# Degree counts moved into the dilation, attention weights prepared first, first convolution tiles filled during the dilation, stores on ACT's queue

## The chip, the cores and the metric

The kernel runs on one core of a Trainium2 chip as a single program. The metric is the device time of the program in microseconds (us). The engines are TensorE (PE; its weight loads are shown apart as PEld), VectorE (DVE), ScalarE (ACT), GpSimd (POOL) and SyncE (SP). DMAs are issued from SP, ACT and POOL, each on a queue of its own.

## What is computed

Sixteen graphs (matrices) of 1024 nodes, with 128 features each, go through four layers. The change touches the first, and the preparation of the second, third and fourth.

```python
# layer 0 for every graph b
h = relu(layernorm(x))
kept = dilate(adj)            # row by row; a row's removals also clear its column
deg = clip(sum(kept, axis=-1), 1, None)
for l in (1, 2, 3):
    agg = (kept @ h) / deg
    o = agg @ Wr[l] + h @ Wx[l] + b[l]
    h = batchnorm(relu(o / norm(o)))      # statistics over all graphs
x = x + concat(h1, h2, h3) @ Wl + bl
# layers 1 to 3, each on relu(layernorm(x)), with the same adj:
#   attention with log(adj) added to the scores (Wq, Wk, Wv, Wo),
#   graph attention (W, a), graph convolution (W, b), each added to x
```

## The kernel before

The program has three stages, each with its own memory pools.

**Dilation** (`dilate_plain`). The sixteen graphs stand in four quarters q of four graphs g each, all in SBUF as fp8 in the tiles `rows` (`M[q]`, 128 partitions x 8 KB per graph). POOL loads them from `adj`, with a cast, in pairs of DMAs (L726, L728), and the loads of later row blocks are gated. For each of eight row blocks s, `rounds(q)` finds the rows' removals by a fixed number of rounds, `DEPTH[s]` (three to nine): TensorE forms ranks in a PSUM bank y, DVE works out thresholds (L775 to L780), TensorE adds them (L828), ACT takes an absolute value (ya, L831), DVE compares (r, L834). A POOL product `pen` (L794) comes first. Each `bulk(q, g)` then applies the result to a graph's row block: TensorE sums (L870), ACT writes `y16` (L872), DVE updates the rows (L880), TensorE turns them (L891 to L894), ACT copies them into the columns (L896). After the last row block, the graph is stored to DRAM as `kept` from SP (L899), 1 MB.

The order is written by `in_order`. Each job is a generator that yields an engine, a duration, the time its input is ready, and a change in a pool of buffers; the planner picks the step that can start first, and records it. The engines' queues hold that order, and every engine works through its queue in order.

**Convolutions** (`convolutions_plain`). SP first loads the weights and vectors wr, wx, Wl, gam, bet, b6 (some twenty DMAs). The first pass, for every graph b, loads x (`xt`), normalises it on DVE, POOL and ACT into `h`, and calls `neighbours(b, h, True)`. That loads the graph's kept matrix into the tile `C`, of which there are two, and forms the degrees with 64 one-column matmuls (L996):

```python
if first:
    ps = pso.tile([P, HN], F32, name="o")[:, :NB]
    ...                       # 64 matmuls of C with ones
    nc.sync.dma_start(rdeg[b].rearrange("(c p) -> p c", p=P), rd[:, 0])
rdb = w2.tile([P, N], F32, name="rdb")
nc.sync.dma_start(rdb, rdeg[b][None, :].to_broadcast([P, N]))
```

The reciprocal degrees `rd` go to DRAM as `rdeg` in single values (L1004), and come back into every partition as `rdb` (L1006). TensorE transposes h (t, L1010; ACT copies it to hT, L1011), `Splitter` cuts h into three bf16 parts on ACT and DVE in turn (L676 to L679; it subtracts in place), and 48 matmuls g (L1021) form the aggregate in two PSUM banks. DVE multiplies each bank by rdb into aggT (L1023), which frees the bank. In two further passes, each layer's output (o, L1061 to L1068) is formed for every graph, and `neighbours` is called again, without the count. In this stage the order is the tile framework's; it lets later work pass where inputs and buffers allow. Tiles h, parts, rdb and xt have two buffers.

**Attentions** (`attentions_plain`). SP loads twelve kinds of weights and vectors, TensorE turns six matrices (L1175), two small products are formed (L1202, L1216), and then a second `in_order` plan runs the three attention layers. Its first work is the sum of x and the convolutions' result (L1328, L1331, from the spilled hT, `h_a`) and the adjacency rows a (SP L1283, ACT L1284).

Of the kernel before, what the change touches and what calls it, by code (L numbers as in the profile page):

```python
# [18 lines left out]
P = 128  # L19
# [681 lines left out]
def dilate_plain(tc, adj, eye, kept, unsettled):  # L701

    nc = tc.nc
    with ExitStack() as ctx:
# [148 lines left out]
        def bulk(q, g):  # L853

            m = M[q]
            for s in range(NB):
# [3 lines left out]
                y16 = bp.tile([P, N], F16, name="y16")  # L860
# [3 lines left out]
                for hf in range(2):  # L864
                    a = max(a, (yield "PE", 0.65, e, ("big", 1)))
# [13 lines left out]
                e = yield "DVE", 1.35, max(e, diagonal), 0  # L879
# [18 lines left out]
                if s == NB - 1:  # L898
                    nc.sync.dma_start(kept[q * G + g], m[:, g])  # L899

        with tc.manual_schedule(engines=set(ENGINES.values())):
            in_order([(9, 1e9, loads())] + [(q, 1e9, rounds(q)) for q in range(4)] + [(q + 100 + g / 9, 1e9, bulk(q, g)) for q in range(4) for g in range(G)],
                     {"big": 5, "y": 3})
# [10 lines left out]
def convolutions_plain(tc, x, eye, kept, rdeg, spill, final, Wr, Wx, bias, gamma, beta, Wl, bl):  # L914
    nc = tc.nc
    with ExitStack() as ctx:
# [3 lines left out]
        ap = ctx.enter_context(tc.tile_pool(name="c_adj", bufs=2))  # L920
# [5 lines left out]
        ident = cp.tile([P, P], F32, name="ident")  # L926
        nc.sync.dma_start(ident, eye)
        minus_half = cp.tile([P, NB], F32, name="minus_half")
        nc.vector.memset(minus_half, -0.5)
        ones = cp.tile([P, P], F32, name="ones")  # L930
        nc.vector.memset(ones, 1.0)
        ones8 = cp.tile([P, 1], F8, name="ones8")
        nc.vector.tensor_copy(ones8, ones[:, 0:1], saturate=False)
# [25 lines left out]
        wr = [matrix(w, f"wr{i}") for i, w in enumerate(Wr)]  # L959
        wx = [matrix(w, f"wx{i}") for i, w in enumerate(Wx)]  # L960
        wl = final[:3]
        for i, t in enumerate(wl):
            nc.sync.dma_start(t, Wl[i * D:(i + 1) * D])
        gam = [column(v, f"gam{i}") for i, v in enumerate(gamma)]
        bet = [column(v, f"bet{i}") for i, v in enumerate(beta)]
        b6 = [row6(v, f"b6_{i}") for i, v in enumerate(bias)]
        last = row6(bl, "bl6")
# [20 lines left out]
        def neighbours(b, h, first):  # L988
# [3 lines left out]
            if first:  # L992
                ps = pso.tile([P, HN], F32, name="o")[:, :NB]
                for i in range(NB):
                    for j in range(NB):
                        nc.tensor.matmul(ps[:, i:i + 1], C[:, j, i * P:(i + 1) * P], ones8, start=j == 0, stop=j == NB - 1)  # L996

                rd = small.tile([P, 2, NB], F32, name="rd")
                nc.vector.tensor_scalar(rd[:, 0], ps, 1.0, None, op0=ALU.max)
                nc.vector.reciprocal(rd[:, 0], rd[:, 0])  # L1000
                nc.vector.tensor_scalar(rd[:, 1], ps, 0.5, None, op0=ALU.is_ge)
                nc.vector.tensor_tensor(rd[:, 0], rd[:, 0], rd[:, 1], op=ALU.mult)
                with nc.allow_non_contiguous_dma(reason="1024 values"):
                    nc.sync.dma_start(rdeg[b].rearrange("(c p) -> p c", p=P), rd[:, 0])  # L1004
# [23 lines left out]
        for b in range(B):  # L1028
            xt = w2.tile([P, NB, D], F32, name="xt")
            nc.sync.dma_start(xt, natural(x[b]))  # L1030
            bs = small.tile([P, NB, 6], F32, name="bs")
            for c in range(NB):
                nc.vector.bn_stats(bs[:, c, :], xt[:, c, :])
            st = small.tile([P, 5, NB], F32, name="ln_st")

            nc.vector.tensor_tensor(st[:, 0], bs[:, :, 1], bs[:, :, 4], op=ALU.add)
            nc.vector.tensor_tensor(st[:, 1], bs[:, :, 1], bs[:, :, 4], op=ALU.subtract)
            nc.vector.tensor_tensor(st[:, 2], bs[:, :, 2], bs[:, :, 5], op=ALU.add)
            nc.vector.tensor_tensor(st[:, 1], st[:, 1], st[:, 1], op=ALU.mult)
            nc.vector.scalar_tensor_tensor(st[:, 2], st[:, 1], 32.0, st[:, 2], op0=ALU.mult, op1=ALU.add)  # L1040
            nc.vector.tensor_scalar(st[:, 2], st[:, 2], 1.0 / D, LN_EPS, op0=ALU.mult, op1=ALU.add)
            rsqrt(st[:, 3], st[:, 2])
            nc.vector.scalar_tensor_tensor(st[:, 4], st[:, 0], -0.5, st[:, 3], op0=ALU.mult, op1=ALU.mult)
            h = w2.tile([P, NB, D], F32, name="h")
            for c in range(NB):
                nc.scalar.activation(h[:, c, :], xt[:, c, :], AF.Relu, bias=st[:, 4, c:c + 1], scale=st[:, 3, c:c + 1])
            neighbours(b, h, True)

        wr_s, wx_s, constant = wr[0], wx[0], row_parts(b6[0], "const0")
        for l in range(3):  # L1050
            stats = kp.tile([P, 2 * B, 6], F32, name="stats")
            for b in range(B):
                if l:
                    rd6 = w2.tile([6, N], F32, name="xt")
                    nc.sync.dma_start(rd6, rdeg[b][None, :].to_broadcast([6, N]))
                    has = w2.tile([6, N], BF16, name="has")
                    nc.vector.tensor_scalar(has, rd6, floor, None, op0=ALU.is_gt)
# [24 lines left out]
                if l < 2:  # L1082
                    neighbours(b, h, False)
                else:
                    for hf in range(2):
                        t = pst.tile([P, HN], F32, name="t")
                        for c in range(4):
                            nc.tensor.transpose(t[:, c * P:(c + 1) * P], h[:, 4 * hf + c, :], ident)
                        nc.scalar.copy(hT[b][:, hf * HN:(hf + 1) * HN], t)
# [49 lines left out]
def attentions_plain(tc, x, spill, final, adj, deg, trouble, eye, Wq, bq, Wk, bk, Wv, bv, Wo, bo, W2, a2, W3, b3, out, scores, bound, reach):  # L1139
    nc = tc.nc  # L1140
    with ExitStack() as ctx:
# [29 lines left out]
        def turned(w, name):  # L1171
            n = w1.tile([P, HN], F32, name="rden")[:, :P]
            nc.sync.dma_start(n, w)
            ps = bank()
            nc.tensor.transpose(ps[:, :P], n, ident)  # L1175
            t = cp.tile([P, P], F32, name=name)
            nc.vector.tensor_copy(t, ps[:, :P])
            return t

        def column(v, name, scale=None):  # L1180
            t = cp.tile([P, 1], F32, name=name)
            with nc.allow_non_contiguous_dma(reason="128 values, once"):
                nc.sync.dma_start(t, v[:, None])
            if scale is not None:
                nc.vector.tensor_scalar(t, t, scale, None, op0=ALU.mult)
            return t

        def everywhere(v, name):
            t = cp.tile([P, D], F32, name=name)
            nc.sync.dma_start(t, v[None, :].to_broadcast([P, D]))  # L1190
            return t

        wq, wk_ = turned(Wq, "wqT"), turned(Wk, "wkT")
        wv, wo, w3 = turned(Wv, "wvT"), turned(Wo, "woT"), turned(W3, "w3T")
        qscale = SCALE / SIGMA
        bqc, bkc, bvc = column(bq, "bq", qscale), column(bk, "bk"), column(bv, "bv")
        bor, b3r = everywhere(bo, "bor"), everywhere(b3, "b3r")

        bv_m = w1.tile([P, HN], F32, name="rden")[:, :P]
        nc.vector.tensor_copy(bv_m, bvc.to_broadcast([P, P]))  # L1200
        ps = bank()
        nc.tensor.matmul(ps[:, :P], bv_m, wo, start=True, stop=True)  # L1202
        nc.vector.tensor_tensor(bor, bor, ps[:, :P], op=ALU.add)

        abd = cp.tile([P, 8], F32, name="abd")
        nc.vector.memset(abd, 0.0)
        with nc.allow_non_contiguous_dma(reason="256 values, once"):
            for h in range(H):
                for k in range(2):
                    nc.sync.dma_start(abd[h * HD:(h + 1) * HD, 4 * k + h:4 * k + h + 1],  # L1210
                                      a2[h, k * HD:(k + 1) * HD][:, None])
        w2T = turned(W2, "w2T")
        w2x = cp.tile([P, D + 8], F32, name="w2x")
        nc.sync.dma_start(w2x[:, :D], W2)
        ps = bank()
        nc.tensor.matmul(ps[:, :8], w2T, abd, start=True, stop=True)  # L1216
        nc.vector.tensor_copy(w2x[:, D:], ps[:, :8])
# [406 lines left out]
def in_order(jobs, pools):  # L1624
# [11 lines left out]
    def tile_of(j):  # L1636
        bank = j["next"][3]
        return bank if isinstance(bank, tuple) else (first, bank)

    while True:  # L1640
        best = None
        for j in jobs:
# [5 lines left out]
            pool, change = tile_of(j)  # L1648
            start = max(free[engine], needs, min(pools[pool]) if change > 0 else 0.0)
# [10 lines left out]
        pool, change = tile_of(j)  # L1660
# [3 lines left out]
        if change > 0:  # L1664
            k = pools[pool].index(min(pools[pool]))
            pools[pool][k] = float("inf")
            j["held"].setdefault(pool, []).append(k)
        elif change < 0:
# [117 lines left out]
```

## Time and profile before

| | us |
|---|---|
| median of three runs | 4152.04 (4149.99 to 4153.77) |
| profiled execution | 4155.19 |
| its span, first to last instruction | 4153.5 |
| last row copy of the dilation ends | 666.4 |
| first g of the convolutions starts | 688.8 |
| last g of the first pass ends | 996.9 |
| last DVE work of the convolutions | 1717.8 |
| first sum L1331 of the attentions | 1738.9 |

| whole span | PE | PEld | DVE | ACT | POOL |
|---|---|---|---|---|---|
| busy us | 3495.4 | 1998.0 | 2531.9 | 2397.5 | 782.0 |
| share | 84% | 48% | 61% | 58% | 19% |

The shares are averages over stages with different limits; what a part of the change is worth is read from its own stage. The page's clock row (PEclk) is the TensorE clock that was granted, as a share of full speed; DMA is the mean busy share of the sixteen DMA engines.

### The profile page before, as it was taken

How to read it: one execution, taken by the hardware profiler on the slowest of the kernel's cores; microseconds unless marked ns; L12 is line 12 of the kernel's file. 1: busy time of each engine (PE TensorE's matmuls, PEld its weight loads, DVE VectorE, ACT ScalarE, POOL GpSimd, SP SyncE). 2: the span in 40 equal slices, each digit the busy share in tenths (PEclk: the TensorE clock that was granted, in tenths of full speed). 3: DMA queues.
4: the chain of work that ended last, by engine and by line, in shares of the span. 5: the costliest groups of instructions: out<-in, count | busy, mean ns of one | idle time of the engine just before them, and what ended most of it. 6: DMA issues, size and time to landing. Idle time of an engine off the chain costs nothing.

```text
span 4153.5 us, 65822 instructions
## 1 busy us (share of the span) xinstructions
PE 3495.4 (84%) x26740; PEld 1998.0 (48%) x26740; DVE 2531.9 (61%) x4783; ACT 2397.5 (58%) x3945; POOL 782.0 (19%) x665
## 2 busy tenths in 40 slices
PE   5888885778999998578889898989988998989775
PEld 3555553345555556433455454545444544544433
DVE  4997773333334443325687678766776767687656
ACT  4777773333333334377657775777676667766540
POOL 7544521100000001111111121111112112111110
PEclk9899986889999999699999998999999999999887
DMA  9532233333332321322112212121222122111000
GB/s 86 33 21 15 14 123 106 112 115 103 134 125 103 124 108 54 118 72 65 53 62 67 77 52 67 67 69 44 67 77 67 47 67 77 52 62 52 26 16 17
DMA packets 212032, 292.12 MB, mean 70 GB/s; under 512 B 93948, under 2 KB 156168, under 8 KB 203528
## 3 DMA queue, kind: packets, MB, share of 16 engines
q1 hardware_dynamic: 127112, 245.61, 18.2%
q0 software_dynamic: 77568, 16.79, 6.7%
q10 hardware_dynamic: 7040, 25.43, 1.5%
q8 instruction: 211, 3.46, 0.3%
q14 instruction: 101, 0.83, 0.1%
HBM read 287.45 MB, written 50.66 MB: 81 GB/s over the span
## 4 chain that ended last, share of the span: by engine, by line
PE 52%; DVE 13%; ACT 6%; DMA 5%; issue 2%; POOL 2%; SPq 0%; ACTq 0%; POOLq 0%; DVEq 0%
PE acc L1418 9%; PE g L1021 8%; PE sum L1544 8%; PE t L1387 5%; PE sum L1598 4%; PE sum L1529 4%; DVE pm L1469 3%; DMA rdeg<-rd 2%; PE o L1067 2%; PE o L1068 2%; PE sum L1331 2%; ACT e L1395 1%; PE sum L1349 1%; DVE rden L1424 1%; PE sum L1269 1%
## 5 line engine op out<-in xcount | busy, mean ns | idle before, releaser
L1395 ACT ACTIVATE e<-t 128x1024 f32<-128x1024 f32 x512 | 507.9, 1022 | 488.1 <-PE t L1387 471.8
L1469 DVE SCALAR_TENSOR_TENSOR pm<-dst,minus,A 128x1024 fp8e4<-128x1024 f32 x512 | 676.1, 1349 | 7.3 <-DMA dst<-scores 7.2
L1021 PE MATMUL g<-C,parts 128*128 128x512 fp8e4 x2304 | 540.8, 390 | 76.4 <-DVE aggT L1023 72.3
L1382 ACT ACTIVATE t<-A 128x2048 f32<-128x2048 fp8e4 x256 | 481.9, 1883 | 3.9 <-ACT dst L1449 0.3
L1544 PEld LDWEIGHTS <-pm 128*128 128x128 fp8e4 x4096 | 347.4, 98 | 186.6 <-issue 164.8
L1544 PE MATMUL sum<-parts,pm 128*128 128x198 bf16 x4096 | 400.7, 251 | 26.2 <-DVE pm L1469 16.2
L1021 PEld LDWEIGHTS <-parts 128*128 128x128 bf16 x2304 | 226.3, 100 | 335.1 <-issue 86.9
L1418 PE MATMUL acc<-e,va 128*32 128x512 f32 x2048 | 332.5, 619 | 41.9 <-ACT e L1395 39.1
L1387 PE MATMUL t<-qT,kT 32*128 32x512 f32 x2048 | 304.9, 666 | 30.5 <-ACT t L1382 30.1
L1418 PE MATMUL acc<-e,ones_hd 128*32 128x512 f32 x2048 | 321.2, 602 | 0.0
L1023 DVE TENSOR_TENSOR aggT<-g,rdb 128x512 f32<-128x512 f32 x96 | 65.5, 690 | 377.1 <-PE g L1021 239.2
L1547 DVE TENSOR_REDUCE pos<-sum 128x132 f32<-128x396 f32 x256 | 144.8, 566 | 201.1 <-PE sum L1544 200.5
L1529 PE MATMUL sum<-parts,A 128*128 128x396 bf16 x1024 | 212.0, 352 | 42.9 <-DVE parts L1521 23.6
L1026 POOL TENSOR_TENSOR nrm<-nrm,minus_half 128x8 f32<-128x8 f32 x48 | 79.5, 1660 | 674.8 <-DVE nrm L1076 674.8
L1598 PE MATMUL sum<-A,gparts 128*128 128x512 fp8e4 x768 | 179.7, 388 | 25.0 <-ACT gparts L1581 17.6
L834 DVE TENSOR_TENSOR r<-ya,both 128x512 bf16<-128x512 f16 x184 | 146.8, 815 | 81.3 <-ACT ya L831 81.2
L1073 ACT ACTIVATE sq<-o 128x512 f32<-128x512 f32 x96 | 55.8, 598 | 227.6 <-PE o L1068 226.3
L880 DVE SCALAR_TENSOR_TENSOR rows<-y,thirty,rows 128x1024 fp8e4<-128x1024 f16 x128 | 171.2, 1347 | 24.5 <-ACT y L872 23.6
L1241 POOL TENSOR_TENSOR ln_st<-ln_st,minus_half 128x8 f32<-128x8 f32 x48 | 86.0, 1792 | 523.3 <-DVE ln_st L1239 389.3
L1529 PEld LDWEIGHTS <-A 128*128 128x128 fp8e4 x1024 | 94.7, 99 | 182.3 <-issue 105.0
L870 PE MATMUL big<-tri,rows 128*128 128x384 fp8e4 (+3 forms) x896 | 174.5, 314 | 1.3 <-ACT H L875 0.6
L883 POOL TENSOR_TENSOR own<-rows,lower 128x256 bf16<-128x256 fp8e4 x128 | 112.8, 891 | 323.7 <-DVE rows L880 229.1
(281 smaller groups left out, 6830.4 us busy)
## 6 DMA issues: line engine op xcount, KB each, us to landing
a<-in_adj_dram SPq DMA_DIRECT2D x128, 512.0 KB
C<-kept SPq DMA_DIRECT2D x48, 1024.0 KB
dst<-scores SPq DMA_DIRECT2D x64, 512.0 KB
rdb<-rdeg SPq DMA_DIRECT2D x48, 512.0 KB
spill<-hT ACTq DMA_DIRECT2D x48, 512.0 KB
kept<-rows SPq DMA_DIRECT2D x16, 1024.0 KB
h_a<-spill SPq DMA_DIRECT2D x64, 256.0 KB
xt<-in_x_dram SPq DMA_DIRECT2D x16, 512.0 KB
```

What stands on the lines that cost most here:

```text
L834: nc.vector.tensor_tensor(r, ya, both[:, 1, :, None].to_broadcast([P, G, P]), op=ALU.is_equal)
L870: nc.tensor.matmul(ps[:, k * P:], lhs, triF[:, :HN - k * P], start=k == 0, stop=k == 3)
L880: nc.vector.scalar_tensor_tensor(row, y16, hh[:, g:g + 1], row, op0=ALU.not_equal, op1=ALU.mult, saturate=False)
L1021: nc.tensor.matmul(ps, parts[:, k, j, :], C[:, j, cols], start=j == 0 and k == 0, stop=j == NB - 1 and k == 2)
L1382: nc.scalar.activation(s, A[b][:, k, None, cols].to_broadcast([P, H, HN]), AF.Copy, scale=16.0)
L1387: nc.tensor.matmul(s[:, hd], kT[r, k * P:(k + 1) * P], qT[r, cols], start=False, stop=True, skip_group_check=True)
L1395: nc.scalar.activation(es[:, hd:hd + 2], s[:, hd:hd + 2], AF.Exp, scale=SIGMA)
L1418: nc.tensor.matmul(ps[r], ones if one else va[:, k, r], es[:, hd], start=k == 0, stop=k == NB - 1)
L1469: nc.vector.scalar_tensor_tensor(pm[:, i, :], dst[hd], minus[:, i, hd:hd + 1], A[b][:, i, :], op0=ALU.is_ge, op1=ALU.mult, saturate=False)
L1529: nc.tensor.matmul(ps[:, :3 * H * W], A[b][:, i, j * P:(j + 1) * P], parts4[:, i, :, :, W:], start=i == 0, stop=i == NB - 1)
L1544: nc.tensor.matmul(ps[:, jj * 6 * W:(jj + 1) * 6 * W], pm[:, i, (j + jj) * P:(j + jj + 1) * P], flat(parts4[:, i, hd]), start=i == 0, stop ...
L1598: nc.tensor.matmul(ps, parts[:, k, m, :], A[b][:, m, cols], start=m == 0 and k == 0, stop=False)
```

## The change

Six things change.

1. The degree count moves to the end of each `bulk(q, g)`: 64 matmuls on the rows in SBUF, four DVE steps, one transpose of the 8 columns, and an ACT copy into `rd_row` (two buffers). `rdeg` is stored from ACT's queue in eight rows of 512 B. `neighbours` no longer counts and only loads `rdb`.
2. `kept` is stored from ACT's queue, not SP's, as each bulk ends.
3. The attention weights are loaded, turned and multiplied at the program's start, by `attention_weights`, on SP, ACT, TensorE and DVE; they go to DRAM as one array `ready_weights`, and the attentions load them with one DMA.
4. The tiles C and xt get pools that are opened ahead of the dilation. C for graphs 0 and 1 and x for graphs 0 and 1 are loaded while the dilation runs, and `norm_first` (job `beside`) normalises graph 0 in place there.
5. The convolutions' weights and vectors are loaded after the second graph's `neighbours` in the program's text, and x is loaded from POOL's queue.
6. `in_order` can take several buffer pools in one step, and the plan counts the six buffers of `y16`.

In the changed program's queues, TensorE has the counts of the first twelve graphs before the last quarter's final rounds, and the last four behind them, two ahead of the last two graphs' turning and two at the end. On SP, the loads of C for graphs 0 and 1 come ahead of wr and wx.

```diff
-                if s == NB - 1:
-                    nc.sync.dma_start(kept[q * G + g], m[:, g])
+            nc.scalar.dma_start(flat(kept[q * G + g]).bitcast(F32), flat(m[:, g]).bitcast(F32))
+            e = yield "PE", 1.8, a, ("big", 1)
+            ps = pp.tile([P, HN], F32, name="big")
+            turned, ps = ps[:NB, P:2 * P], ps[:, :NB]
+            for i in range(NB):
+                for j in range(NB):
+                    nc.tensor.matmul(ps[:, i:i + 1], m[:, g, j, i * P:(i + 1) * P], ones8[:, 0:1], start=j == 0, stop=j == NB - 1)
+            e = yield "DVE", 0.7, e, 0
+            rd = sp.tile([P, 2, NB], F32, name="rd")
...
+            e = yield "PE", 0.2, e, 0
+            nc.tensor.transpose(turned, rd[:, 0], ident)
+            yield "ACT", 0.3, e, ("big", -1)
+            row = sp.tile([NB, P], F32, name="rd_row", bufs=2)
+            nc.scalar.copy(row, turned)
+            nc.scalar.dma_start(rdeg[q * G + g].rearrange("(c p) -> c p", p=P), row)
...
-                    a = max(a, (yield "PE", 0.65, e, ("big", 1)))
+                    a = max(a, (yield "PE", 0.65, e, [("big", 1), ("y16", 1 - hf)]))
+                    if hf == 0:
+                        y16 = bp.tile([P, N], F16, name="y16")
...
-                     {"big": 5, "y": 3})
+            in_order([(9, 1e9, loads()), (1000, 1e9, beside)] + ...,
+                     {"big": 5, "y": 3, "y16": 6})
...
+def norm_first(tc, x, pool, h, minus_half):
+    nc.sync.dma_start(h, natural(x[0]))
+    t = yield "DVE", 3.2, 50.0, 0
...
+    yield "ACT", 2.3, t, 0
+    for c in range(NB):
+        nc.scalar.activation(h[:, c, :], h[:, c, :], AF.Relu, bias=st[:, 4, c:c + 1], scale=st[:, 3, c:c + 1])
...
         for b in range(B):
+            if b == 0:
+                h = h0
+            else:
+                xt = xp.tile([P, NB, D], F32, name="xt")
+                nc.gpsimd.dma_start(xt, natural(x[b]))
...
-            neighbours(b, h, True)
+            neighbours(b, h)
+            if b == 1:
+                wr = [matrix(w, f"wr{i}") for i, w in enumerate(Wr)]
+                wx = [matrix(w, f"wx{i}") for i, w in enumerate(Wx)]
...
+def attention_weights(tc, rp, ident, into, Wq, bq, Wk, bk, Wv, bv, Wo, bo, W2, a2, W3, b3):
...
+        for k, w in enumerate((Wq, Wk, Wv, Wo, W3, W2)):
+            (nc.sync, nc.scalar)[k % 2].dma_start(raw[:, k], w)
...
+        for k in range(6):
+            ps = pp.tile([P, P], F32, name="turn")
+            nc.tensor.transpose(ps, raw[:, k], ident)
+            nc.vector.tensor_copy(t[:, k * D:(k + 1) * D] if k < 5 else w2T, ps)
...
+        nc.sync.dma_start(into, t)
...
+        weights = cp.tile(list(ready_weights.shape), F32, name="weights")
+        nc.sync.dma_start(weights, ready_weights)
...
-        dilate_plain(tc, adj, eye, kept, unsettled)
+        ready_weights = dp.tile([P, 8 * D + 10], F32, name="ready_weights")
...
+            with tc.tile_pool(name="early", bufs=1) as yp, tc.tile_pool(name="c_adj", bufs=2) as ap, \
+                    tc.tile_pool(name="c_x", bufs=2) as xp:
...
+                attention_weights(tc, ap, ident, ready_weights, *weights)
+                dilate_plain(tc, adj, eye, kept, rdeg, unsettled, norm_first(tc, x, yp, h0, minus_half))
+                convolutions_plain(tc, x, ident, ap, xp, h0, minus_half, kept, rdeg, spill, final, *layer0)
```

## The prediction

> **What bounds the kernel now.** I read the table of stages first, then the chain of waits in the stage it singled out, then single instructions. The program has three stages: the dilation (0 to 667 us), the convolutions (to 1718) and the attentions. 0.2% of 4152 us is 8.3 us, about what a measurement of this kernel can tell from no change. Busy time by stage, all columns being engine busy us (with counts), granted clock, DMA share and GB/s:
>
> ```profile
> core 0: us, PE busy (x) PEld busy (x) DVE busy (x) ACT busy (x) POOL busy (x), PEclk, DMA share, GB/s
> 0.00:680.00 680.00, 510.61 (x5672) 346.03 (x5672) 499.73 (x1438) 452.56 (x889) 309.32 (x407) 0.89 0.48 53
> 680.00:1000.00 320.00, 241.87 (x1954) 129.41 (x1955) 109.44 (x399) 103.47 (x225) 25.72 (x16) 0.84 0.40 112
> 1000.00:1320.00 320.00, 302.46 (x1684) 182.56 (x1684) 124.69 (x227) 120.40 (x298) 31.64 (x20) 0.97 0.34 122
> ```
>
> From 1000 on TensorE is busy 302 of 320 us at clock 0.97: the second pass is bound by it. The first pass, 680 to 1000, is not: 242 of 320 us at clock 0.84, and no other engine is half busy. The chain of waits from 800 to 1020 says why:
>
> ```profile
> 817.87 0.20 DVE bs L1033
> 818.08 0.08 DVE rd L1002
> 818.17 10.28 DMA rdeg<-rd
> 828.46 4.33 DMA rdb<-rdeg
> ...
> 834.71 9.12 DMA rdeg<-rd
> ...
> 856.89 10.54 DMA rdeg<-rd
> 867.45 4.22 DMA rdb<-rdeg
> ...
> 873.59 10.39 DMA rdeg<-rd
> ```
>
> Each matrix's reciprocal degrees go to DRAM in about 10 us and come back in 4.3, and TensorE waits for aggT behind them. Two matrices take 38.5 us (g restarts at 837.59 and at 876.04). The waits agree: who waited, for whom, total us, times, longest.
>
> ```profile
> DVE aggT L1023 <- DMA rdb<-rdeg: 129.8, 14, 14.2
> ```
>
> Two more places matter, each in the timeline. The last row block of the dilation is copied at 666.4, the first g starts at 688.76. And in the attentions' start, SP issues 27 small loads and TensorE turns weights before the first sum L1331:
>
> ```profile
> 1718.11 0.33 SPq L1156 DMA_DIRECT2D ident<-in_eye_dram  x1
> ...
> 1730.20 0.90 SPq L1283 DMA_DIRECT2D a<-in_adj_dram  x2
> ...
> 1738.94 1.22 PE L1331 MATMUL sum<-final,h_a 128*128 128x128 f32 x4
> ```
>
> **What the Trainium skill says.** DMA: Bandwidth & Descriptors, Specifications, asks for at least 512 B per transfer for line rate. The trace agrees: 4 KB in pieces of 4 B takes about 10 us, the 512 KB broadcast 4.3. Its section on queues, rings and completion order says descriptors of one ring are consumed in order; so an rdeg store issued on ACT behind 1 MB kept stores waits for them. No run so far shows that. TensorE: Matmul & The Clock Gate, HAM oscillation, says idle gaps throw the clock back; the trace agrees (0.84 with the gaps, 0.97 without).
>
> **The change, part by part** (the sum is against the profiled execution, 4155.19 us; its span is 4153.5 and 1.7 lie around it. The median of the runs is 3.15 lower).
>
> *First pass: -103 (-80 to -128).* Before, first g to last g runs from 688.76 to 996.88, 308 us. Removed are 16 counts of 64 matmuls (1.74 us each) and the round trip inside the pass. In the changed instruction order two matrices form a unit: 96 matmuls g (44 took 9.50 us at full clock, 0.216 each: 20.7) and 16 transposes (8 took 0.87: 1.7), so 22.5 us if TensorE never waits. It will, once a unit: transposes read h, DVE subtracts in place after them, ACT casts, then g goes on. Without the rdb wait the trace's own sequence (872.51 to 876.04) costs 3.5 us, of which 2 are work counted above. ACT's order adds about 1: the next unit's h wait for statistics that stand behind aggT. I take 25 us a unit: 8 x 25 + 5 for a cold start = 205. Best is 8 x 22.5 = 180, worst 28.5 a unit = 228. Nothing else fills a unit: by the same trace DVE needs about 14 and ACT 13.5. C, rdb and x are 4 MB per unit, 160 GB/s, where 263 were moved at share 0.64 (600 to 620). x moves to POOL's queue, where one such issue costs about 0.9 us (L728); POOL is idle over 85% there.
>
> *Counts in the dilation: +15 (0 to 30).* Sixteen counts stay on TensorE, 1.74 us each plus a transpose. Twelve stand, in its order, before the last quarter's final rounds: 23 us. Idle time there is about 3.5 us (575 to 600, busy 86%) and 5 (600 to 617), so about 15 remain; it adds to the bound engine of a serial chain, and can do no better than vanish in the chain's own gaps. ACT gets 32 DMA issues at 0.33 us (as L1090) and 16 copies at 0.3; between 600 and 620 it is busy 18.2 of 20, so I count this cover as gone: part of the 15, its excess in the upper end. DVE's 0.7 us per count and h0 (3 us on DVE, 3.2 on ACT, 1.7 on POOL) fall in its 80 to 90% busy time: likewise. The buffer rule for y16 only orders; no ACT y waited for DVE in this trace, so 0 (-2 to 2, inside the ends).
>
> *Dilation start: +4 (0 to 10).* Weights, their store (0.5 MB) and two x are 2.1 MB, while row loads run at full DMA: pairs of 0.98 MB every 2.52 us (12.18, 14.71, 17.23), 390 GB/s. If all collides, 5.5 us, plus 640 pieces of 4 B. The engines' part is hidden: the first real product waits for pen on POOL until 29.6, and the weights should be turned by then. Without that cover it would cost what it exceeds.
>
> *Dilation end: +4 (0 to 6).* Two counts (3.5 us) stand on TensorE ahead of the last two matrices' transposes.
>
> *Start of the convolutions: -10 (-4 to -13).* 22.4 us from last copy to first g become about 12. C for matrices 0 and 1 and h for 0 lie ready, and about 20 small SP loads no longer precede them. What is late next: ACT's hT waits for all four last kept stores, since the new tiles lie where the rows were. Before, four stores issued 662.1 to 666.4 had landed by 674.5, 8 us after the last. Then hT, casts and subtractions, 4 us. The last two counts hide under the stores. wr and wx are not needed in the first units; SP passes 4 of them ahead of rdb, which is wanted half a g later.
>
> *Attentions' start: -9 (0 to -14).* 27 loads become 1; the a loads move from 1730.2 to about 1721.5, 0.43 us per issue. L1331 can move 13, so the adjacency stream sets 9. If later due work absorbs the head start it is 0.
>
> Sum: -103 + 15 + 4 + 4 - 10 - 9 = -99, 4056 profiled, **median 4053**. All good ends together give 3997, all bad ends 4114.
>
> **Rivals.** *TensorE-bound pass, chance 0.13.* The unit costs 22.5 and the chain's idle gaps absorb the counts: -128 + 0 + 4 + 4 - 10 - 9 = -139, median 4013. For it: 0.97 in the second pass. Against: the in-place subtraction above, with only two parts buffers.
>
> *The next wait, chance 0.10.* C has two buffers; a refill starts when g of the one before ends, and behind it queue rdb on SP. If C and rdb take 14 us instead of the 6 the trace shows (issue 738.61, first use 744.8), a unit costs 32: 256 + 5 is a saving of 47 instead of 103, median 4109.
>
> *Slower, chance 0.05: ACT stands at rd_row.* That tile has two buffers, so 14 of the 16 copies wait for the rdeg store two back, queued on ACT behind kept stores. While ACT stands, every ya and row copy behind it stands, and the last quarter's chain with it. The gain of 99 is gone at 7.1 us per copy; at 8.5 (119 us) the median is 4172. Against: four kept stores took 12.4 us, 3.1 each, mostly one or two stand ahead, and ACT has some 6 us of other work between.
>
> *It does nothing, 0.01:* only if the rdeg store still precedes each rdb in the pass.
>
> **Numbers.** Forecast 0.71, TensorE-bound 0.13, next wait 0.10, slower 0.05, nothing 0.01. Faster is 0.94, same 0.01, slower 0.05. The likeliest case's own ends are 3997 and 4114, each only if every term falls the same way; 4005 to 4110 holds both faster rivals and about 8 in 10.
>
> **What would show it.** In the changed profile: no chain through DMA rdeg in the convolutions; first g about 13 us after the last rows copy; units of 25 us; clock above 0.9 in the pass; last rows copy at about 690 rather than 666. A unit above 30 with waits on C, or long waits of rd_row for rdeg in ACT, would prove a rival; an attentions stage that ends as long after its start as before, but starts no earlier relative to the last layer, would void the -9.

## The result, and the profile after

The changed kernel takes **4034.64 us** (median of four runs, 4027.68 to 4039.04) against 4151.01 before: a ratio of 0.9719, with a 95% interval of 0.9702 to 0.9737, some 116 us saved where 99 were forecast. Its profiled execution took 4039.04 us, with a span of 4037.3, 116.2 under that of before. By stages, from the two profiled executions (us):

| | before | after | difference | forecast |
|---|---|---|---|---|
| last row copy of the dilation ends | 666.4 | 686.9 | +20.5 | +23 |
| from there to the first g | 22.4 | 7.3 | -15.1 | -10 |
| first g to the end of the pass's 768th g | 308.1 | 204.4 | -103.7 | -103 |
| from there to the last DVE work of the convolutions | 720.9 | 712.3 | -8.6 | 0 |
| the rest | 2435.7 | 2426.5 | -9.2 | -9 |

The table of stages of the changed kernel, with the same columns as before:

```profile
core 0: us, PE busy (x) PEld busy (x) DVE busy (x) ACT busy (x) POOL busy (x), PEclk, DMA share, GB/s
560.00:620.00 60.00, 55.40 (x981) 43.58 (x978) 39.58 (x135) 35.66 (x73) 10.21 (x14) 0.72 0.56 209
620.00:687.00 67.00, 48.93 (x678) 33.88 (x675) 29.18 (x95) 30.00 (x60) 9.87 (x10) 0.66 0.18 71
700.00:900.00 200.00, 190.70 (x937) 95.03 (x936) 102.83 (x324) 100.47 (x226) 37.58 (x29) 0.97 0.46 159
900.00:1152.00 252.00, 243.19 (x1345) 148.03 (x1344) 97.35 (x165) 97.60 (x240) 24.56 (x15) 0.98 0.36 128
```

In the first pass TensorE is now busy 190.7 of 200 us at clock 0.97, where it was 242 of 320 at 0.84; from 760 to 900 every 20 us slice is full. The price stands in the first row: from 560 to 620 TensorE is busy 55.4 of 60 us at a clock of 0.72, where the kernel before had 49.4 at 0.93. The chain of waits from 700 to 800 holds no rdeg. In its place, at the start of the pass alone, stands x:

```profile
725.33 6.96 DMA xt<-in_x_dram
732.32 1.66 DVE bs L1055 x8
735.01 1.67 POOL ln_st L1045
...
737.85 1.18 DVE bs L1055 x6
...
741.88 0.69 DVE aggT L1042
742.62 0.58 PE g L1040
...
747.04 20.33 PE g L1040 x92
...
771.02 19.86 PE g L1040 x92
```

The columns are start, duration, and what the chain went through. This load of x takes 7 us (the median of all is 4.9); its statistics (bs) stand on DVE ahead of aggT, which TensorE waits for; from 747 on g follows g. The timeline shows the steady units, two matrices each, 23.5 us apart:

```profile
794.65 20.02 PE L1040 MATMUL g<-C,parts 128*128 128x512 fp8e4 x92
...
818.15 20.02 PE L1040 MATMUL g<-C,parts 128*128 128x512 fp8e4 x92
```

The waits from 690 to 900 (total us, times, longest) say the same of the whole pass: the 129.8 us of aggT behind rdb are gone, DVE waits 31.7 us for x, and TensorE loses 9.2 us to aggT.

```profile
DVE bs L1055 <- DMA xt<-in_x_dram: 31.7, 11, 6.1
...
PE g L1040 <- DVE aggT L1042: 9.2, 3, 4.1
```

The timeline shows the two starts: that of the convolutions, and that of the attentions, whose last DVE work of the stage before ended at 1611.

```profile
686.32 0.59 ACT L898 CAST rows<-big 128x512 fp8e4<-128x512 f32 x1 [0.48 <-ACT rows L898]
...
692.50 1.07 ACT L1030 COPY hT<-t 128x512 f32<-128x512 f32 x2 [2.87 <-DMA kept<-rows]
...
693.47 1.15 ACT L676 CAST parts<-xt 128x512 bf16<-128x512 f32 x2
...
694.15 1.03 PE L1040 MATMUL g<-C,parts 128*128 128x512 fp8e4 x2 [2.49 <-DMA wr<-in_L_gnn_Wr_dram]
...
1617.91 1.06 ACT L1310 ACTIVATE A<-a 128x1024 fp8e4<-128x1024 f32 x1 [14.02 <-DMA a<-in_adj_dram]
```

The first g stands 7.3 us behind the end of the last row copy; 2.9 of these are hT's wait, which ACT has ahead of the casts (parts), for the last kept store. The trace puts the first g's own wait down to wr, which g doesn't read; what g needs is the first cast, and it is through at that time. In the attentions ACT's first adjacency block comes 7.1 us after the stage before, where it took 17.4 (1735.2 against 1717.8).

### The profile page after: what moved, and what is told of

Read it like the earlier page. It is cut to its first block, busy times and chain, and to the rows that moved or that the text cites. A ratio compares the mean times of both kernels' runs of the same rounds, so it can differ in the third digit from the quotient of the medians.

```text
span 4037.3 us, 65855 instructions
## 1 busy us (share of the span) xinstructions
PE 3474.4 (86%) x26756; PEld 1998.6 (50%) x26756; DVE 2527.9 (63%) x4782; ACT 2401.7 (59%) x3961; POOL 794.7 (20%) x680
## 4 chain that ended last, share of the span: by engine, by line
PE 58%; DVE 15%; ACT 7%; DMA 3%; issue 2%; POOL 2%; ACTq 0%; SPq 0%; POOLq 0%; DVEq 0%
PE g L1040 12%; PE acc L1444 9%; PE sum L1570 9%; PE t L1413 5%; PE sum L1624 4%; PE sum L1555 4%; DVE pm L1495 3%; PE o L1093 2%; PE sum L1357 2%; PE o L1094 2%; PE sum L1375 1%; ACT e L1421 1%; DVE rden L1450 1%; PE t L1029 1%; PE sum L1295 1%
## 5 line engine op out<-in xcount | busy, mean ns | idle before, releaser
L1040 PE MATMUL g<-C,parts 128*128 128x512 fp8e4 x2304 | 521.3, 381 | 15.4 <-DVE aggT L1042 9.2
L1413 PE MATMUL t<-qT,kT 32*128 32x512 f32 x2048 | 307.7, 672 | 31.7 <-ACT t L1408 31.3
L1624 PE MATMUL sum<-A,gparts 128*128 128x512 fp8e4 x768 | 178.0, 385 | 24.9 <-ACT gparts L1607 17.6
L1106 ACT ACTIVATE h<-o,nrm 128x128 f32<-128x128 f32 x384 | 105.7, 384 | 116.9 <-POOL nrm L1045 113.7
```

What stands on the lines that cost most here:

```text
L1040: nc.tensor.matmul(ps, parts[:, k, j, :], C[:, j, cols], start=j == 0 and k == 0, stop=j == NB - 1 and k == 2)
L1413: nc.tensor.matmul(s[:, hd], kT[r, k * P:(k + 1) * P], qT[r, cols], start=False, stop=True, skip_group_check=True)
L1624: nc.tensor.matmul(ps, parts[:, k, m, :], A[b][:, m, cols], start=m == 0 and k == 0, stop=False)
```

## The experiments

How much single executions differ is read from kernels that have a stage in common. The kernel before and row_store run the same instructions in the dilation, and its last row copies end at 666.4 in the first and at 660.9 in the second:

```profile
665.20 1.21 ACT L896 CAST rows<-big 128x512 fp8e4<-128x512 f32 x2 [0.54 <-PE big L891]
...
659.72 1.21 ACT L896 CAST rows<-big 128x512 fp8e4<-128x512 f32 x2 [0.53 <-PE big L891]
```

The three kernels with the changed dilation untouched (changed, x_four, after_again) end it at 686.9, 688.5 and 689.0. The first pass took 204.4 us in one execution of the changed kernel and 208.2 in the other. So a difference of up to 5.5 us at the last row copy, or 4 us in the pass, between two traces doesn't show an effect. The ratio of the changed kernel to the kernel before was 0.9719 in one set of runs and 0.9688 in another; ratios are compared inside one set of runs, and the first two sets below had no run of the changed kernel. The last three columns are when the last row copy ends, the first g starts and the convolutions end in the profiled execution:

| kernel | ratio to before | last row copy | first g | convolutions' end |
|---|---|---|---|---|
| before | 1 | 666.4 | 688.8 | 1717.8 |
| changed | 0.9719 (0.9702 to 0.9737) | 686.9 | 694.2 | 1610.8 |
| first set: row_store | 0.9796 (0.9778 to 0.9813) | 660.9 | 683.5 | 1633.6 |
| counts_back | 0.9905 (0.9887 to 0.9923) | 667.2 | 669.0 | 1706.8 |
| no_counts | 0.9634 (0.9607 to 0.9662) | 669.5 | 671.3 | 1583.6 |
| weights_back | 0.9730 (0.9713 to 0.9748) | 679.6 | 688.3 | 1604.1 |
| second set: stores_sp | 0.9686 (0.9660 to 0.9711) | 677.1 | 685.9 | 1602.3 |
| x_late | 0.9694 (0.9678 to 0.9710) | 681.9 | 689.9 | 1606.4 |
| x_four | 0.9699 (0.9683 to 0.9716) | 688.5 | 695.8 | 1614.2 |
| counts_late | 0.9689 (0.9672 to 0.9705) | 681.4 | 690.1 | 1609.4 |
| third set: after_again | 0.9688 (0.9675 to 0.9701) | 689.0 | 697.0 | 1612.8 |
| sp_xlate | 0.9652 (0.9639 to 0.9665) | 677.6 | 686.7 | 1610.2 |
| sp_xlate_clate | 0.9677 (0.9664 to 0.9690) | 678.3 | 687.2 | 1609.0 |
| sp_xlate_wlate | 0.9678 (0.9665 to 0.9691) | 681.5 | 690.1 | 1609.4 |

**row_store: the kernel before, with the store of the reciprocals in rows.**

```diff
+                turned, ps = ps[:NB, P:2 * P], ps[:, :NB]
...
-                    nc.sync.dma_start(rdeg[b].rearrange("(c p) -> p c", p=P), rd[:, 0])
+                nc.tensor.transpose(turned, rd[:, 0], ident)
+                row = small.tile([NB, P], F32, name="rd_row")
+                nc.scalar.copy(row, turned)
+                nc.sync.dma_start(rdeg[b].rearrange("(c p) -> c p", p=P), row)
```

> This is the kernel before with one edit: the reciprocal degrees are turned by TensorE and stored as 8 rows of 512 B instead of 1024 pieces of 4 B; counts and loads stay in the first pass. Theory A, the 4-byte pieces are most of the cost: the store falls from 10 us to about 2.5, the trip of some 7 us then lies beside the 10 us of g of the matrix before, and the first pass falls from 308 us to about 225 (it keeps 16 counts of 1.74 us), median about 4068. Theory B, any trip between two g costs, since it starts late: one wait of some 7 us stays per unit of two matrices, the pass takes about 265 us, median about 4108.

The first pass fell from 308.1 to 233.9 us, and the median by some 87. SP's timeline shows the trip, store and load in turn:

```profile
764.49 0.28 SPq L1007 DMA_DIRECT2D rdeg<-rd_row  x1
767.80 0.32 SPq L1009 DMA_DIRECT2D rdb<-rdeg  x1
...
780.88 0.30 SPq L1007 DMA_DIRECT2D rdeg<-rd_row  x1
782.15 0.33 SPq L1009 DMA_DIRECT2D rdb<-rdeg  x1
```

In all sixteen graphs the load is issued 1.2 to 3.3 us after the store, where 8.2 to 11.7 lay between. Where aggT waited 129.8 us for rdb in the pass, 18.8 are left (both from the waits, from 680 to 1000 and from 680 to 920). With the counts still in it, the pass now keeps TensorE busy:

```profile
core 0: us, PE busy (x) PEld busy (x) DVE busy (x) ACT busy (x) POOL busy (x), PEclk, DMA share, GB/s
760.00:900.00 140.00, 132.60 (x1205) 71.31 (x1204) 62.24 (x207) 61.83 (x142) 11.46 (x7) 0.99 0.42 141
```

So theory A holds, with a pass 9 us longer than it said: 74.2 of the 103.7 us that the change gains in the pass come from the form of the store alone, with the counts and the trip left where they were. The Trainium skill (DMA: Bandwidth & Descriptors, Specifications) asks for 512 B or more per transfer; here the trace agrees: from the store's issue to the load's, the same 4 KB take some 2 us in rows of 512 B and some 10 in pieces of 4 B.

**counts_back: the changed kernel, with the counts in the pass again, in 4 B pieces.**

```diff
-            e = yield "PE", 1.8, a, ("big", 1)
-            ... # count, reciprocals, transpose, copy and rdeg store of bulk()
+            if first:
+                ... # as in the kernel before: 64 matmuls of C, rd, rdeg on SP
```

> This is the changed kernel with the counts put back into the first pass, stored in 4-byte pieces on SP; C, x and h of the first matrices stay prefetched, the kept stores stay on ACT's queue, and the weights stay ready. Theory A, moving the counts is the change's whole gain in the pass: the pass is back at about 300 us, the dilation ends some 14 us earlier (last row copy near 673), median about 4115 to 4125. Theory B, the prefetched tiles and the short list of loads on SP carry a good part of it: median under 4080.

The pass took 316.4 us, no less than before, and the median lay at 4121.9, as theory A had it: the prefetched tiles carry only the start, which is even shorter here (1.8 us from the last row copy to the first g). But this edit brings back two things at once, the counts and the store in 4 B pieces, and row_store shows that most of the loss is the store. So it doesn't show that moving the counts is the gain. The dilation ended at 667.2, with its first dT at 57.0. That is level with the kernel before (666.4, first dT at 50.5), but 6.3 us behind row_store (660.9, first dT at 50.7); whether the late start is absorbed stays open.

**no_counts: the changed kernel without the counts.**

```diff
-            e = yield "PE", 1.8, a, ("big", 1)
-            ... # count, reciprocals, transpose and copy
-            nc.scalar.dma_start(rdeg[q * G + g].rearrange("(c p) -> c p", p=P), row)
+            nc.scalar.dma_start(rdeg[q * G + g].rearrange("(c p) -> c p", p=P), even)
```

> This is the changed kernel without the counts: their 16 x 64 matmuls, the reciprocals, the transposes and the copies are left out, and every stored reciprocal is the constant 1/32; the stores stay. It sizes the counts in the dilation. Theory A, as in the prediction: they cost about 10 us in the body and 4 at the tail, so the last row copy is near 673 instead of 687 and the median near 4021. Theory B, the gaps absorb them and the later end comes from the later start: the last row copy stays at 682 or later, median 4030 to 4035.

`even` holds the constant 1/32, so the stages after the first pass see other values than in the changed kernel.

```profile
core 0: us, PE busy (x) PEld busy (x) DVE busy (x) ACT busy (x) POOL busy (x), PEclk, DMA share, GB/s
560.00:620.00 60.00, 43.65 (x413) 28.17 (x413) 39.35 (x102) 41.21 (x82) 12.94 (x17) 0.87 0.61 230
620.00:670.00 50.00, 31.45 (x234) 17.89 (x232) 18.40 (x63) 19.59 (x36) 4.25 (x5) 0.60 0.13 50
```

Beside the rows of the changed kernel: TensorE does 75 us of work there instead of 104, and the last dT comes at 653.1 instead of 669.3. In these two traces the counts cost 16.2 us up to the last dT, 17.4 up to the last row copy, and 22.9 up to the first g (671.3 against 694.2), more than theory A had. Counted from the first kept store, where the counts begin, the last row copy ends after 112.7 us without them and after 127.2 with them, the latter in both executions of the changed kernel. The last 5.5 are order, as ACT's timeline in this kernel shows:

```profile
669.38 0.63 ACT L676 CAST parts<-xt 128x512 bf16<-128x512 f32 x1
...
678.24 1.07 ACT L1015 COPY hT<-t 128x512 f32<-128x512 f32 x2 [5.27 <-DMA kept<-rows]
```

Here the casts stand on ACT ahead of hT, so hT's wait of 5.3 us for the kept stores holds nobody, and g starts 1.8 us after the last row copy. In the changed kernel the casts stand behind it. The span is 37.7 us shorter than that of the changed kernel, 27.2 of it by the convolutions' end; the attentions, which see other values here, took 2416 us instead of 2426.5. That part stays open.

**weights_back: the attentions' weights loaded in the attentions again.**

```diff
-                attention_weights(tc, ap, ident, ready_weights, *weights)
...
-        nc.sync.dma_start(weights, ready_weights)
+        wq, wk_ = turned(Wq, "wqT"), turned(Wk, "wkT")
+        ... # and the rest, as in the kernel before
```

> This is the changed kernel with the attentions' weights loaded and turned at the attentions' start, as before. Theory A: the attentions' start costs 9 us more and the dilation begins some 3 us earlier (first dT near 53.5 instead of 56.9), of which nothing or little is left at its end: median about 4041. Theory B, a later start of the dilation carries to its end: 9 minus 3, median about 4038, and the last row copy 3 us earlier than 687. Theory C, the adjacency stream sets the attentions' start: within 3 us of 4035.

The ratio, 0.9730, overlaps the 0.9719 of the changed kernel's first runs and lies above the 0.9688 of the third set; as these are different sets of runs, they don't settle which is faster. The trace shows two opposite effects. The attentions' first adjacency block comes 15.7 us after the stage before, instead of 7.1:

```profile
1619.79 1.06 ACT L1351 ACTIVATE A<-a 128x1024 fp8e4<-128x1024 f32 x1 [22.63 <-DMA a<-in_adj_dram]
```

And the dilation's first dT comes at 51.8 instead of 56.9, its last row copy 7.3 us earlier, the way theory B had it. The early weights gain 8.6 us at the attentions' start and cost 5.1 us at the first dT, where the changed dilation's three executions lie within 0.6 us (56.6 to 57.2). How much of that is left at the dilation's end can't be read from one trace, when two executions of one dilation end 5.5 us apart.

**x_late: the first x issued on ACT at 100 us of planned work.**

```diff
-    nc.sync.dma_start(h, natural(x[0]))
-    t = yield "DVE", 3.2, 50.0, 0
+    t = yield "ACT", 0.4, 100.0, 0
+    nc.scalar.dma_start(h, natural(x[0]))
+    t = yield "DVE", 3.2, t + 8.0, 0
```

> This is the changed kernel with one edit: the first matrix's x is issued on ACT's queue, after about 100 us of the dilation's planned work, instead of on SP at 14 us. Theory A, this 512 KB is what holds up the row loads between 20 and 28 us (two of them 4.9 us apart instead of 2.5) and a late start is carried to the dilation's end: first dT near 52 instead of 56.9, last row copy near 682 instead of 687, median some 5 us under the changed kernel's. Theory B, the weights' loads and turns hold it up: first dT stays at 56 or later and nothing is gained.

The first dT came at 56.1, as theory B had it: x doesn't set the start. The last row copy came 5.0 us earlier, as theory A had it, but two executions of one dilation lie as far apart, so a gain isn't shown. The edit does more than move x: the plan orders the later work differently (the first kept store is issued at 568.8 instead of 559.7), and the statistics of x leave DVE's first 100 us (39 us of its work from 30 to 100 become 35).

**x_four: four tiles for x in the first pass.**

```diff
-                xt = xp.tile([P, NB, D], F32, name="xt")
+                xt = (xp, w2)[b // 2 % 2].tile([P, NB, D], F32, name=("xt", "h")[b // 2 % 2])
...
-                h = w2.tile([P, NB, D], F32, name="h")
+                h = xt
```

> This is the changed kernel with x's norm written in place, so that four tiles of x rotate in the first pass instead of two of x and two of h. Theory A, the cold start of the pass waits for x, whose refill stands behind h's release: the third x is issued near 692 instead of 698, the fourth near 693 instead of 704, and the stretch from the first g to the start of the steady units, 694 to 747 now, shrinks from 53 us to about 44; median some 9 us lower. Theory B, the cold start is set by ACT's and DVE's own order of work, or by the clock: it stays at 50 us or more, and the median within 3 us.

The wait for x went, and others came:

```profile
711.43 0.38 PE L1040 MATMUL g<-C,parts 128*128 128x512 fp8e4 x1
718.47 0.58 PE L1040 MATMUL g<-C,parts 128*128 128x512 fp8e4 x1 [6.66 <-DVE aggT L1042]
...
763.72 7.03 PE L1040 MATMUL g<-C,parts 128*128 128x512 fp8e4 x24 [2.22 <-DVE aggT L1042]
```

The second unit took 25 us instead of 32, but the first one waited 6.7 us for aggT, and later units wait for aggT too; the pass took 207.9 us, as in the second execution of the changed kernel. Its ratio doesn't stand apart from the others of its set. The cold start isn't the refill of x alone: DVE's order of work, with statistics of later graphs and DVE's waits of 1.4 to 1.6 us for POOL ahead of aggT, gives the next wait.

**stores_sp: the kept and rdeg stores on SP.**

```diff
-            nc.scalar.dma_start(flat(kept[q * G + g]).bitcast(F32), flat(m[:, g]).bitcast(F32))
+            nc.sync.dma_start(flat(kept[q * G + g]).bitcast(F32), flat(m[:, g]).bitcast(F32))
...
-            nc.scalar.dma_start(rdeg[q * G + g].rearrange("(c p) -> c p", p=P), row)
+            nc.sync.dma_start(rdeg[q * G + g].rearrange("(c p) -> c p", p=P), row)
```

> This is the changed kernel with the kept and rdeg stores issued on SP instead of ACT. Theory A, the other queue is what lets C be fetched early: on SP the two C loads stand behind the last kept stores, so that they start near 690 instead of 564, and the first g comes some 5 us after 694; ACT is freed of 32 issues of about 0.33 us; median within 5 us of the changed kernel's or a few us above. Theory B, the ACT issues are on the dilation's chain: last row copy some 5 to 10 us before 687, median lower by that.

Theory A is wrong: SP takes the C loads between the stores, at 565 and 580 us in its timeline.

The last row copy comes at 677.1, 9.8 us earlier than in the changed kernel, as theory B had it, but not all of that is the moved issues. Up to the first kept store both kernels run the same instructions, and this execution is 4.7 us ahead there:

```profile
554.98 2.30 SPq L900 DMA_DIRECT2D kept<-rows  x2
```

In the changed kernel:

```profile
559.69 0.35 ACTq L900 DMA_DIRECT2D kept<-rows  x1
```

From there to the end of the last row copy it takes 122.1 us, where both executions of the changed kernel take 127.2. So 5.1 us are left for the move of the issues. What an issue costs ACT is seen in two pieces of its timeline. With the stores on SP the next copy starts 0.14 us after the small copy of rd_row:

```profile
604.12 0.24 ACT L917 COPY rd_row<-big 8x128 f32<-8x128 f32 x1
604.26 0.57 ACT L898 CAST rows<-big 128x512 fp8e4<-128x512 f32 x1
```

In the changed kernel:

```profile
612.01 0.24 ACT L917 COPY rd_row<-big 8x128 f32<-8x128 f32 x1
612.28 0.29 ACTq L918 DMA_DIRECT2D rdeg<-rd_row  x1
612.62 0.59 ACT L898 CAST rows<-big 128x512 fp8e4<-128x512 f32 x1 [0.36 <-ACT rd_row L917]
```

This issue takes 0.29 us, and ACT's next copy starts after it is through: 0.61 us from the start of one copy to the start of the next, with ACT idle for 0.36. The Trainium skill (DMA: Bandwidth & Descriptors, Issuing engines are not separate DMA queues) says that issuing from several engines saves only issue time on the sequencer; here the move to ACT spent it on an engine that the dilation's chain goes through.

**counts_late: the twelve early counts held back, in halves.**

```diff
+            while q < 3 and (3, NB - 1) not in begun:
+                yield
-            e = yield "PE", 1.8, a, ("big", 1)
+            e = yield "PE", 0.95, a, ("big", 1)
...
+                if i == NB // 2:
+                    e = yield "PE", 0.95, e - HOP, 0
```

> This is the changed kernel with the twelve counts of the first three quarters held back until the last quarter's last round has begun, each in two halves of 32 matmuls, so that they stand in the gaps of that serial chain, where TensorE is busy 12 of 20 us. Theory A, a count costs what it adds to a busy TensorE: in the gaps, some 2 us in each of nine rounds of the chain, 18 of the 28 us vanish, and the last row copy is near 677 instead of 687; median some 9 us lower. Theory B, in the chain each count's reciprocals and copies on DVE and ACT and the longer gap delay the next step as well: last row copy at 687 or later.

```profile
core 0: us, PE busy (x) PEld busy (x) DVE busy (x) ACT busy (x) POOL busy (x), PEclk, DMA share, GB/s
620.00:640.00 20.00, 20.00 (x510) 17.78 (x508) 7.75 (x47) 3.72 (x10) 0.00 (x0) 0.59 0.02 5
```

The last row copy came at 681.4, 5.5 us earlier, where theory A had 10 and theory B none; two executions of one dilation differ by as much, so neither is shown. The gaps were overfilled: the plan put 96 count matmuls into each step of the chain, TensorE is busy 20 of 20 us there, and a step takes 5.2 us where the steps after the last count take 3.1. At the convolutions' end 1.4 us are left.

**after_again, and three combinations.** The edits are those above; sp_xlate_wlate also turns the weights into a planned job, behind a fill of their tile at 100 us of planned work.

> The changed kernel itself, so that the three kernels of this call stand beside it on one chip: 0.972 of the kernel before, as its runs showed, last row copy at 687, first g at 694.

> The changed kernel with the kept and rdeg stores on SP and the first x issued late on ACT. Theory A, the two gains are of different stretches and add up: last row copy some 14 us before 687, near 673, the first g near 681, the median some 13 us under the changed kernel's. Theory B, both only shift the order of work in the last rounds of the dilation, each gives the other's gain: near 677, median 8 us under.

sp_xlate is faster than the changed kernel in the same set of runs: 4026.2 against 4040.3 us, and the intervals of their ratios don't meet. It has the lowest ratio of all versions that compute the same. Its last row copy comes at 677.6, where stores_sp alone had 677.1 and theory A 673; with single traces 5.5 us apart this leans to theory B without settling it. Its profiled span is 11.2 us shorter than that of after_again, of which 2.6 arose by the convolutions' end and 8.6 in the attentions, which the edit doesn't touch. So the lower time is shown, its full cause isn't.

> As the kernel with stores on SP and a late first x, and the twelve early counts held back into the last chain's gaps. Theory A, the counts' matmuls still cost on the busy stretch: 4 us less again, last row copy near 669. Theory B, with ACT freed of the issues the counts are cheap where the change put them, and the held-back counts lengthen the chain: last row copy 5 us or more after that of the kernel without them held back.

> As the kernel with stores on SP and a late first x, and the attentions' weights loaded and turned within the dilation, behind a fill of their tile at about 100 us of planned work, instead of before it. Theory A, what the start loses is the time of the weights' and x's pieces in the DMA engines beside the row loads: with both moved the first dT is near 51 instead of 56.9, and the last row copy 5 us before that of the kernel without this; median some 18 us under the changed kernel's. Theory B, the later work on DVE, TensorE and SP costs in the busy stretch what the start gains: no difference of more than 2 us at the last row copy.

Neither adds to sp_xlate; both medians lie above its own (4033.1 and 4036.1 us). Held-back counts left the last row copy about where it was (678.3), between both theories. Late weights brought the first dT to 51.0, as theory A had it, but the last row copy didn't come earlier (681.5): the start's gain isn't seen at the end. The 3.9 us by which it came later are less than two executions differ by.

## Why the prediction was right, and where its steps were off

The direction held, and so did the mechanism, that the round trip of the reciprocal degrees holds up the first pass. The measured time lies in the range; the forecast saving was 17 us too small. Some of the terms were right by luck.

- **First pass, -103: measured -103.7, but from two errors that cancel.** The units were put at 25 us, of which 2.5 were a wait of TensorE. In the trace they follow each other at 23.5 (794.65, 818.15, 841.65) with no wait, and that includes some output products: the next unit's casts are done while g runs. The cold start was put at 5 us. At 23.5 a unit the pass would take 188; it took 204.4, so the cold start costs about 16. In the trace x and its statistics on DVE hold it up; x_four, without the wait for x, had other waits and no shorter pass. The second execution of the changed kernel took 208.2 us with the same steady units, so the agreement with -103 to the microsecond is luck. The TensorE-bound rival was right for the steady units, and wrong in that the counts would vanish. The next-wait rival named the right kind of wait, but C: g never waited for C; x was late, and only in the first two units.
- **What the -103 consists of** the prediction took as one removal. The form of the store alone gives 74.2 (308.1 to 233.9). The other 29.5 are, by size, the counts' own TensorE time, 16 x 1.74 = 27.8; and the dilation pays 22.9 of them up to the first g. By this sum the move itself is worth some 7 us, and with the second execution's 208.2 us in the pass and first g at 697.0 nothing is left of it. So it isn't shown that moving the counts gains anything over storing them in rows; no run had the changed kernel's start with the counts in the pass and the store in rows, which would measure it.
- **Counts, +15, and dilation end, +4: 16.2 up to the last dT, and from there to the last row copy 17.6 us instead of 13.5 (+4.1).** The first is sized well, from a sum of TensorE's time. (The prediction read 5 us of idle time from 600 to 617; TensorE is busy 13.2 of these 17 us, so it is 3.8. The 15 stays.) That ACT's issues are part of it was said: from the first kept store to the last dT stores_sp takes 105.8 us, where both executions of the changed kernel take 109.6. Behind the last dT the prediction named the two counts alone. With the counts and the stores on SP that stretch takes 16.4 us, with the kept stores on ACT but no counts (counts_back) 14.8. So some 2.8 of the 4.1 us are the counts and 1.3 are ACT's issues, a term that it put at nothing there.
- **Dilation start, +4: 6.4 at the first dT (50.5 to 56.9).** What is left of it at the dilation's end isn't shown. The last dT of no_counts, which starts as late, comes at 653.1; with the early start it came at 652.9 in the kernel before and at 647.7 in row_store. Against the first nothing is left, against the second nearly all.
- **Convolutions' start, -10: measured -15.1, past the good end of the range (-13).** The step that failed is its price after the stores: 8 us for the landing and 4 behind it. The stores landed 5.5 us after the last row copy; hT waited for them, the casts follow in 1 us, and g starts before the subtractions are through.
- **The rest of the convolutions, 0 expected: measured -8.6.** It was left out. In the changed kernel 40 recorded output products (L1093, L1094) run inside the first pass, instead of 10; 30 at 0.11 us are 3.3 us that the second pass no longer has. Around the end of the first layer TensorE's waits fell from 7.0 us (1249 to 1261) to 3.0 (1161 to 1164). The remaining 1.3 us are less than single executions differ by: this stretch took 716.2 us in row_store, which has the code of before there, and 707.7 in the second execution of the changed kernel.
- **Attentions' start, -9: measured -9.2.** The adjacency stream set it, as reasoned: 7.1 us to the first block, and the sums, which start at 2.6, no longer the last.
- **The slower rival is refuted.** ACT waited once, 0.6 us, for an rdeg store; 7.1 us per copy would have been needed. No run shows how long an rdeg store stood behind kept stores. ACT did cost time, by issuing rather than by standing.

## What to carry to other kernels

Before moving a slow round trip, look at the size of its pieces: storing 1024 values in eight rows gave seven tenths of the pass's gain without moving anything. A store put on another engine's queue costs that engine its issue and the overlap of its neighbours, so put it on an engine that the chain doesn't pass through. Before a gain of a few us is read from one trace, compare two executions of the same instructions; here they lay up to 5.5 us apart at the end of one stage. A pass that becomes bound by TensorE still has a cold start, and its price is the first refills and what stands ahead of them on the in-order engines.

## What was not expected of the hardware

- A DMA issue on ACT takes 0.28 to 0.74 us and breaks the overlap of ACT's instructions: two copies that follow at 0.14 us stand 0.61 apart with an issue between. With 32 issues moved to SP the stretch from the first kept store to the last row copy took 122.1 us instead of 127.2.
- Count matmuls of one column take 0.027 us each, 1.74 per 64; in the stretch they fill, the granted clock was 0.72 instead of the 0.87 without them, with TensorE busy 55.4 instead of 43.7 of 60 us. In counts_late TensorE was busy 20.0 of 20 us at a clock of 0.59. The prediction read a low clock as a matter of idle gaps; in these stretches the fuller TensorE had the lower one. Why is open.
- With the weights ready and the same values, the attentions took from 2421 to 2430 us over ten profiled executions of kernels that differ only ahead of them; a gain of some us in another stage is read from that stage, not from the total.
